# One block of each expert at fixed places first: the routed tail of a cross-attention and mixture-of-experts kernel

## The chip, the core and the metric

The kernel runs on one core of a Trainium2 chip. The metric is the device time of one execution in microseconds (us), as the median of several runs. Besides the runs there is one profiled execution, whose trace shows every instruction of the five engines: TensorE (PE), VectorE (DVE), ScalarE (ACT), GpSimd (POOL) and SyncE (SP), the last of which only issues transfers (DMA).

## The reference, cut to what matters

The reference is a layer over 8 images of 512 rows of width 256. A first half (cross-attention that keeps the top scores, a modulated long convolution, an MLP) gives a new `x`. The second half, which the change is about, is a mixture of 8 experts of which each row takes one, beside a shared expert:

```
logits = x @ gate_w                       # 8 experts
top_id = argmax(logits);  score = sigmoid(max(logits))
xs = x * score
y_e = (silu(xs @ rt_gate[e]) * (xs @ rt_up[e])) @ rt_down[e]     # only e = top_id is used
out = x_in + tanh(g_ffn) * (shared_swiglu(x) + y_{top_id})
```

Each expert has three weight matrices of 512 KB (`rt_gate`, `rt_up`, `rt_down`), all in float32.

## The kernel before, in words

**Recording and order.** The kernel does not issue its instructions as it is written. Calls go through proxies of the engines into a planner (`Plan`), which notes cost, inputs, outputs and buffers of each operation. `Plan.order()` then makes a greedy list schedule: at each step it takes the operation that can start first by its model, and among those ready the one noted earliest. That schedule is issued in one go, so the order on each engine, SP among them, is fixed when the kernel is built. All recorded instructions carry the helper's line L323; transfers that need a register carry the lines of their own functions.

**Stages.** For image `b`, `prepare` and `attention` run beside `behind(b - 1)`, which does `mixed` (the long convolution: products `pfi`, `pxf`, `pfo`, `py` on PE, with sums `yf` on POOL) and `after_mix` (the MLP of the first half, the router, the shared expert) of the image before. The last image has no attention beside it; `attended` is true from there on.

**The routed rows.** `after_mix` scatters the rows of an image, in four indirect transfers of 128 rows from POOL, into a table `xtab` in HBM in which every expert has its own stretch of `CAP` rows. `blocks_of` counts on DVE how many whole blocks of 128 rows each expert has that are not done yet (`pdone`), and writes for `TAKE[b]` blocks which expert (`blk[b][:, 0]`) and which first row (`blk[b][:, 1]`) each has. `block` then does one block. It loads 128 rows (`xb`, L1282, with a register for the first row, L1281) and three weight matrices (`load_w`, L1295, with a register for the expert, L1293), transposes the rows (`pxb`), multiplies (`pg`, `pu`), applies silu and product (`sgr`, `ger`), multiplies by `rt_down` (`pyr`), scales (`yb` on ACT), and adds the result to the rows of `out` with an indirect accumulating transfer from POOL (`out_dram<-yb,to`). Two such accumulations touch the same tensor, so each waits for the one before it to land. In `routed`, the `pyr` part of a block is put behind the first part of the next block.

**The end.** Image 6 leaves four blocks (called 6_0 to 6_3 below); 6_0 is put beside `mixed(7)`, the other three between the MLP and the shared expert of image 7. When image 7 is scattered, `blocks_of` with `all_` true rounds up, so that all rows left are covered, and the last 15 blocks (`TAKE[7]`) run alone. If more than 15 were needed (`few`), a general path at the end would do everything again. From `attended` on, the weights of a block don't go to the pool of five weight buffers but to the attention's buffers, which are free by then:

```
room = ((pq, "s"), (pk, "e"), (pk, "acc")) if attended else ((wpool, "w"),) * 3
```

`pq` has four buffers of the tag `s`, `pk` has two of each tag. So four gate matrices, two up matrices and two down matrices can be held.

Of the kernel before, what the change touches and what calls it, by code (L numbers as in the profile page):

```python
# [16 lines left out]
I32 = mybir.dt.int32  # L17
AF = mybir.ActivationFunctionType
ALU = mybir.AluOpType
# [3 lines left out]
P = 128  # L23
# [320 lines left out]
def tile_kernel(ctx: ExitStack, tc: tile.TileContext, a: dict, out: bass.AP):  # L344
    nc = tc.nc
    x, cx = a["x"], a["ctx_768"]
    B, T, D = x.shape
# [5 lines left out]
    NE, _, NI = a["L0_ffn_rt_gate"].shape  # L353
# [12 lines left out]

    CAP = B * T + P
    DX = D + 1  # L370
    NBLK = B * T // P + NE - 1
    FIRST = 1
    TAKE = {b: NF for b in range(FIRST + 1, B - 1)}
    TAKE[FIRST] = NF * (FIRST + 1) - 5
    TAKE[B - 1] = NBLK - 1 - sum(TAKE.values())

    const = ctx.enter_context(tc.tile_pool(name="const", bufs=1))
    wpool = ctx.enter_context(tc.tile_pool(name="wpool", bufs=5))
    pa = ctx.enter_context(tc.tile_pool(name="pa", bufs=1))
    pk = ctx.enter_context(tc.tile_pool(name="pk", bufs=2))  # L380
    pq = ctx.enter_context(tc.tile_pool(name="pq", bufs=4))
# [7 lines left out]
    plan = Plan(nc)  # L389
    V, S, GP, TE, SY = (plan.engine(n, e) for n, e in (  # L390
        ("DVE", nc.vector), ("ACT", nc.scalar), ("POOL", nc.gpsimd), ("PE", nc.tensor), ("SP", nc.sync)))
# [7 lines left out]
    def bank2(name):  # L399
        return bank(name, ps_ac, "ac")  # L400
# [135 lines left out]
    capse = const.tile([P, NE], F32, name="capse")  # L536
    blim = const.tile([P, 2, NBLK], F32, name="blim")
    tid = const.tile([P, B * NT], I32, name="tid")
    xtab = dr.tile([NE * CAP + P, DX], F32, name="xtab")

    cum = const.tile([P, NE], BF16, name="cum")
    pdone = const.tile([P, NE], F32, name="pdone")

    pre = const.tile([P, 4, 2 * NE], F32, name="pre")
    base = const.tile([P, NE + 1], F32, name="base")
    blk = {b: const.tile([P, 2, n], I32, name=f"blk{b}") for b, n in TAKE.items()}
    few = const.tile([P, 1], F32, name="few")
    free = const.tile([P, NE], I32, name="free")
    for t_ in (cum, pdone, pre):
# [2 lines left out]
    GP.memset(blim[:, 0], float(NE - 1))  # L552
    GP.memset(blim[:, 1], float(NE * CAP))

# [49 lines left out]
    def setup():  # L604
# [16 lines left out]
        GP.memset(zrow[:, D : D + 1].bitcast(I32), 1 << 20)  # L621
        q.dma_start(xtab[NE * CAP :, :], zrow)
        yield
# [9 lines left out]
        GP.tensor_scalar(iotap, ioc, float(P), None, ALU.mult)  # L633
        GP.tensor_scalar(capse, iota8, float(CAP), None, ALU.mult)
        GP.tensor_copy(iotab, ioc)
# [463 lines left out]
    def after_mix(b, s, between=()):  # L1099
# [11 lines left out]
        acc = accs(f"am{b}")  # L1111
# [46 lines left out]
        E = V if b == B - 1 else GP  # L1158
# [8 lines left out]
        V.tensor_tensor(oh, bc(iota8, 1, NT), bc(fx[:, 0], 2, NE), ALU.is_equal)  # L1167
        E.tensor_scalar(fx[:, 1], fx[:, 0], float(CAP), None, ALU.mult)

# [19 lines left out]
        for t in range(NT):  # L1189
            GP.indirect_dma_start(out=xtab[:], out_offset=bass.IndirectOffsetOnAxis(ap=ix_[:, t : t + 1], axis=0),  # L1190
                                  in_=hx[:, t, :], in_offset=None)
        if b in TAKE and not general:
            blocks_of(E, blk[b], TAKE[b], b == B - 1)
        yield

        acc = accs(f"ae{b}")
# [25 lines left out]
    def blocks_of(E, to, n, all_):  # L1222

        pc = bank(f"pcnt_{to.name}")
        TE.matmul(pc[:, :NE], ones16, cum, start=True, stop=True)
        w_ = pk.tile([P, 2, NE], F32, tag="bw", name=f"bw_{to.name}", bufs=1)
        nb, di = w_[:, 0, :], w_[:, 1, :]
        S.activation(nb, pc[:, :NE], AF.Copy, scale=1.0 / P)
        E.tensor_scalar(nb, nb, (63.5 if all_ else -63.5) / P, MAGIC, ALU.add, ALU.add)
        E.tensor_scalar(nb, nb, MAGIC, None, ALU.subtract)  # L1230
        E.tensor_sub(pre[:, 0, NE:], nb, pdone)
        for i in range(3):
            E.tensor_add(pre[:, i + 1, NE:], pre[:, i, NE:], pre[:, i, NE - 2 ** i : 2 * NE - 2 ** i])
        en, st = pre[:, 3, NE:], pre[:, 3, NE - 1 : 2 * NE - 1]
        if all_:
            V.tensor_scalar(few, en[:, NE - 1 :], float(n), None, ALU.is_le)
        V.tensor_scalar(en, en, float(n), None, ALU.min)

        E.tensor_sub(base[:, :NE], pdone, st)
        E.tensor_scalar(base[:, :NE], base[:, :NE], float(P), None, ALU.mult)  # L1240
        E.tensor_add(base[:, :NE], base[:, :NE], capse)
        E.tensor_sub(di, base[:, 1:], base[:, :NE])
        E.tensor_sub(nb, en, st)
        E.tensor_add(pdone, pdone, nb)
        cm = pk.tile([P, 2, n, NE], F32, tag="t2", name=f"cm_{to.name}")
        V.tensor_tensor(cm[:, 0], bc(iotab[:, :n], 2, NE), bc(en, 1, n), ALU.is_ge)
        E.tensor_mul(cm[:, 1], cm[:, 0], bc(di, 1, n))
        rd = pk.tile([P, 2, n], F32, tag="rd", name=f"rd_{to.name}", bufs=1)
        V.tensor_reduce(rd, cm, AX.X, ALU.add)
        E.tensor_scalar(rd[:, 1], rd[:, 1], base[:, 0:1], None, ALU.add)  # L1250
        E.tensor_add(rd[:, 1], rd[:, 1], iotap[:, :n])
        V.tensor_tensor(to, rd, blim[:, :, :n], ALU.min)
# [24 lines left out]
    def rows_of(bl, i, n, tag="xb"):  # L1277
        xb = pk.tile([P, DX], F32, tag=tag, name=f"xb{n}")

        def load():  # L1280
            r = nc.sync.value_load(bl[0:1, 1, i : i + 1], min_val=0, max_val=NE * CAP)  # L1281
            nc.sync.dma_start(xb, xtab[bass.ds(r, P), :])  # L1282

        plan.note_dma("SP", load, xb, [bl, xtab])
        return xb

    def block(bl, i, n, xb=None):

        if xb is None:
            xb = rows_of(bl, i, n)  # L1290

        def load_w(w, m):
            e = nc.sync.value_load(bl[0:1, 0, i : i + 1], min_val=0, max_val=NE - 1)  # L1293
            ap = a["L0_ffn_rt_" + m][bass.ds(e, 1)].rearrange("o k n -> (o k) n")
            nc.sync.dma_start(w, ap.rearrange("(c p) n -> p c n", p=P))  # L1295


        room = ((pq, "s"), (pk, "e"), (pk, "acc")) if attended else ((wpool, "w"),) * 3
        ws = []
        for m, k, (pool, tag) in zip(("gate", "up", "down"), (ND, ND, NIC), room):  # L1300
            t_ = pool.tile([P, 1024], F32, tag=tag, name=f"rt_{m}{n}")
            ws.append(t_.rearrange("p (c n) -> p c n", c=k))
            plan.note_dma("SP", partial(load_w, ws[-1], m), ws[-1], [bl])
        wg, wu, wd = ws
        to = pk.tile([P, 1], I32, tag="to", name=f"to{n}", bufs=3)
        GP.tensor_copy(to, xb[:, D : D + 1].bitcast(I32))
        p_ = bank(f"pxb{n}")
        for c in range(ND):
            TE.transpose(p_[:, c * P : (c + 1) * P], xb[:, c * P : (c + 1) * P], ident)
        xT = pk.tile([P, ND, P], F32, tag="xbT", name=f"xbT{n}")  # L1310
        S.copy(xT.rearrange("p c t -> p (c t)"), p_[:, : ND * P])
        p1, p2 = bank(f"pg{n}"), bank(f"pu{n}")
        for p_, w in ((p1, wg), (p2, wu)):
            for k in range(NIC):
                for c in range(ND):
                    TE.matmul(p_[:, k * P : (k + 1) * P], w[:, c, k * P : (k + 1) * P], xT[:, c, :],
                              start=(c == 0), stop=(c == ND - 1))
        sg = pk.tile([P, T], F32, tag="sg", name=f"sgr{n}")
        S.activation(sg, p1, AF.Silu)
        ga = pk.tile([P, T], F32, tag="ga", name=f"ger{n}")  # L1320
        V.tensor_mul(ga, sg, p2)

        def down():
            py = bank2(f"pyr{n}")
            for k in range(NIC):
                TE.matmul(py[:, :D], ga[:, k * P : (k + 1) * P], wd[:, k, :],
                          start=(k == 0), stop=(k == NIC - 1))
            yb = pk.tile([P, D], F32, tag="yb", name=f"yb{n}")
            S.activation(yb, py[:, :D], AF.Copy, scale=scal[:, 2:3])
            GP.indirect_dma_start(out=orows, out_offset=bass.IndirectOffsetOnAxis(ap=to, axis=0),  # L1330
                                  in_=yb, in_offset=None, bounds_check=B * T - 1, oob_is_err=False,
                                  compute_op=ALU.add)
        return down

    def routed(b, i0, i1, rows=None):
        late = None
        for i in range(i0, i1):
            now = block(blk[b], i, f"{b}_{i}", rows and rows[i])
            if late is not None:
                late()  # L1340
            late = now
            if i + 1 == i1:
                late()
            yield

# [12 lines left out]
    def together(*parts):  # L1358
        for _ in beside(*parts):
            pass  # L1360
# [12 lines left out]
    attended = general = False  # L1373
# [25 lines left out]
        pass  # L1399
    attended = True  # L1400
    together(behind(B - 1))
    together((routed(B - 1, 0, TAKE[B - 1]), 1))

    plan.issue(tc)

# [12 lines left out]
    with tc.If(rows_ok < P):  # L1418
# [10 lines left out]
        for b in range(B):  # L1429
            s = St()  # L1430
# [51 lines left out]
```

## Time and profile before

| | |
|---|---|
| median of 3 runs | 1792.7 us (1792.55 to 1793.37) |
| the profiled execution's own time | 1794.11 us |
| its span, first to last instruction | 1792.3 us |
| PE busy | 1513.1 us (84%) |
| DVE, ACT, POOL busy | 1302.1, 1154.6, 931.5 us |
| granted TensorE clock, mean | 0.874 |
| moved by DMA | 131.68 MB, mean 73 GB/s |
| DMA in the third last and second last of 40 slices | 228 and 280 GB/s |
| issues of rt_gate, rt_up, rt_down | 38 each, 512 KB |
| out_dram<-yb,to on POOL | 38 |

The shares of busy time are means over stages that are bound by different engines. The change works in the last 250 us of the span alone, so what counts is what ends last there: the table's whole-span figures only say how large that part is.

### The profile page before, as it was taken

The page shows a single profiled execution, that of the slowest core. Times are in us where ns is not written, and L with a number is a line of the kernel's source. Part 1 is how long each engine was busy: PE and PEld are TensorE (multiplying, and loading weights), DVE is VectorE, ACT ScalarE, POOL GpSimd, SP SyncE. Part 2 cuts the span into 40 slices and gives each one's busy share as a digit, 9 for nine tenths or more (in the row PEclk, how much of TensorE's full clock was granted, in tenths as well). Part 3 has the DMA queues.
Part 4 walks back from the last instruction along what each step waited for, and adds up shares of the span by engine and source line. Part 5 has one row for each costly group of instructions (what it writes and reads, how often), then busy time and mean ns, then how long its engine had stood idle before and what let it go on. Part 6 is the DMA issues. An engine that isn't in the chain of part 4 may idle for free. (4 is left out here: it accounts for less than half of the span.)

```text
span 1792.3 us, 21191 instructions
## 1 busy us (share of the span) xinstructions
PE 1513.1 (84%) x6363; PEld 893.1 (50%) x6363; DVE 1302.1 (73%) x3073; ACT 1154.6 (64%) x2008; POOL 931.5 (52%) x1072
## 2 busy tenths in 40 slices
PE   5365577797998798999889999998999989889885
PEld 2143333344543454465436554654465547547685
DVE  6989977885878697977798889697978987222210
ACT  4778844676747774887578877885788678123121
POOL 5578544445363645465555765474557646233122
PEclk8555677786998799998989999998999989989898
DMA  4000110001200120143103330431033205523794
GB/s 118 0 1 24 33 35 18 12 12 47 70 20 12 47 65 18 36 128 96 54 12 109 91 102 12 135 107 58 12 111 107 66 12 162 179 103 86 228 280 117
DMA packets 101289, 131.68 MB, mean 73 GB/s; under 512 B 9687, under 2 KB 73004, under 8 KB 101166
## 3 DMA queue, kind: packets, MB, share of 16 engines
q1 hardware_dynamic: 93102, 121.05, 21.1%
q0 software_dynamic: 7008, 8.42, 2.6%
q8 instruction: 52, 0.85, 0.2%
q10 hardware_dynamic: 1056, 0.79, 0.1%
q14 instruction: 71, 0.58, 0.1%
HBM read 112.22 MB, written 18.78 MB: 73 GB/s over the span
## 5 line engine op out<-in xcount | busy, mean ns | idle before, releaser
L323 PE MATMUL pS<-kT,qT 32*128 32x512 f32 x512 | 285.6, 742 | 71.2 <-DVE mn L323 61.0
L323 POOL TENSOR_TENSOR acc<-acc,e 128x1024 f32<-128x1024 f32 x96 | 229.0, 2385 | 182.3 <-ACT e L323 179.9
L323 DVE MAX8 top<-mn 128x8 f32<-128x256 f32 (+1 forms) x512 | 276.0, 556 | 11.9
L323 ACT COPY sc<-pS 128x512 f32<-128x512 f32 x256 | 145.6, 584 | 167.1 <-PE pS L323 136.9
L323 DVE SCALAR_TENSOR_TENSOR e<-sc,t,e 128x1024 f32<-128x1024 f32 x128 | 180.3, 1421 | 40.6 <-ACT e L323 40.3
L323 DVE TENSOR_TENSOR mn<-sc,pS 128x512 f32<-128x512 f32 x256 | 165.2, 677 | 35.9 <-PE pS L323 19.9
L323 POOL TENSOR_TENSOR mn<-mn 128x256 int32<-128x256 int32 x128 | 102.4, 800 | 164.4 <-DVE hi L323 163.8
L323 PEld LDWEIGHTS pS<-kT,qT 32*128 32x128 f32 x512 | 75.9, 208 | 203.6 <-DVE mn L323 98.9
L323 ACT ACTIVATE e<-sc,sm 128x1024 f32<-128x1024 f32 x128 | 145.1, 1146 | 16.1 <-POOL acc L323 13.2
L323 ACT ACT_TABLE_LOAD x118 | 151.4, 1283 | 4.0 <-issue 2.0
L323 PE MATMUL pm<-hT,w 128*128 128x512 f32 x256 | 137.9, 677 | 13.6 <-ACT hT L323 13.6
L323 ACT ACTIVATE junk<-sc,sm 128x1024 bf16<-128x1024 f32 x128 | 146.1, 1141 | 1.3
L323 PEld LDWEIGHTS pu<-aT,cx 128*96 128x96 f32 x1024 | 122.2, 168 | 28.6 <-issue 24.1
L323 PE MATMUL pu<-aT,cx 128*96 128x128 f32 x1024 | 135.4, 282 | 0.2 <-ACT aT L323 0.2
L323 PE MATMUL am<-w,ga 128*128 128x256 f32 x512 | 129.1, 398 | 6.1 <-ACT ga L323 6.1
L323 PEld LDWEIGHTS am<-w,ga 128*128 128x128 f32 x512 | 96.9, 196 | 51.4 <-issue 27.6
L323 POOL DMA_INDIRECT out_dram<-yb,to x38 | 61.5, 1620 | 96.7 <-DMA out_dram<-yb,to 46.3
L323 ACT ACTIVATE e<-e,sm 128x1024 f32<-128x1024 f32 x96 | 108.5, 1147 | 1.6 <-DVE sm L323 1.6
L323 POOL TENSOR_TENSOR mn<-mn,hi 128x256 int32<-128x256 int32 x128 | 104.9, 819 | 8.0
L323 DVE TENSOR_TENSOR ger<-sgr,pu 128x512 f32<-128x512 f32 x38 | 26.0, 684 | 108.7 <-PE pu L323 105.9
L323 DVE MATCH_REPLACE8 mn<-top,mn 128x256 f32<-128x256 f32 x256 | 104.6, 409 | 0.0
L323 POOL TENSOR_TENSOR yf<-yf,t 128x512 f32<-128x512 f32 (+1 forms) x80 | 85.2, 1089 | 35.0 <-DVE t L323 33.7
(287 smaller groups left out, 3125.0 us busy)
## 6 DMA issues: line engine op xcount, KB each, us to landing
rt_gate<-in_L_ffn_rt_gate_dram SPq DMA_DIRECT2D x38, 512.0 KB
rt_up<-in_L_ffn_rt_up_dram SPq DMA_DIRECT2D x38, 512.0 KB
rt_down<-in_L_ffn_rt_down_dram SPq DMA_DIRECT2D x38, 512.0 KB
w<-in_L_xattn_W_dram SPq DMA_DIRECT2D x32, 512.0 KB
cx<-in_ctx_dram SPq DMA_DIRECT2D x7, 768.0 KB
xtab<-zt SPq DMA_DIRECT2D x8, 642.5 KB
xb<-xtab SPq DMA_DIRECT2D x38, 128.5 KB
xt<-in_x_dram SPq DMA_DIRECT2D x8, 512.0 KB
```

The lines of the kernel that those rows point to most:

```text
L323: o.fn()
```

## The change

The 15 blocks at the end become 8 + 7. The first eight are one block for each expert, `own`: expert `e` at its first row not done yet, `pdone * P + e * CAP`. That is known when image 6 has been counted. Which expert comes when is fixed, so their weights are loaded by plain transfers without a register; only their rows need one. `pdone` goes up by one for each expert, `blocks_of` clips negative counts at zero, and the other seven blocks are routed as before. In every block after `attended`, the up and the down matrix now alternate between two tags (`e` and `mn`, `acc` and `kT`), so four of each can be held. This holds for the blocks 6_0 to 6_3 too, whose buffers come from the same tags.

```diff
-    TAKE[B - 1] = NBLK - 1 - sum(TAKE.values())
+    TAKE[B - 1] = NBLK - 1 - sum(TAKE.values()) - NE
...
+    own = const.tile([P, NE], I32, name="own")
...
         if b in TAKE and not general:
+            if b == B - 1:
+                V.scalar_tensor_tensor(own, pdone, float(P), capse, ALU.mult, ALU.add)
+                E.tensor_scalar(pdone, pdone, 1.0, None, ALU.add)
             blocks_of(E, blk[b], TAKE[b], b == B - 1)
...
         E.tensor_sub(pre[:, 0, NE:], nb, pdone)
+        if all_:
+            V.tensor_scalar(pre[:, 0, NE:], pre[:, 0, NE:], 0.0, None, ALU.max)
...
-            r = nc.sync.value_load(bl[0:1, 1, i : i + 1], min_val=0, max_val=NE * CAP)
+            first = own[0:1, i : i + 1] if bl is own else bl[0:1, 1, i : i + 1]
+            r = nc.sync.value_load(first, min_val=0, max_val=NE * CAP)
...
-        room = ((pq, "s"), (pk, "e"), (pk, "acc")) if attended else ((wpool, "w"),) * 3
+        room = ((pq, "s"), (pk, ("e", "mn")[i % 2]), (pk, ("acc", "kT")[i % 2])) if attended else ((wpool, "w"),) * 3
...
-            plan.note_dma("SP", partial(load_w, ws[-1], m), ws[-1], [bl])
+            if bl is own:
+                SY.dma_start(ws[-1], a["L0_ffn_rt_" + m][i].rearrange("(c p) n -> p c n", p=P))
+            else:
+                plan.note_dma("SP", partial(load_w, ws[-1], m), ws[-1], [bl])
...
     def routed(b, i0, i1, rows=None):
+        yield from blocks([(blk[b], i, f"{b}_{i}", rows and rows[i]) for i in range(i0, i1)])
+
+    def blocks(all_):
         late = None
-        for i in range(i0, i1):
-            now = block(blk[b], i, f"{b}_{i}", rows and rows[i])
+        for one in all_:
+            now = block(*one)
...
-    together((routed(B - 1, 0, TAKE[B - 1]), 1))
+    together((blocks([(own, e, f"o_{e}", None) for e in range(NE)]
+                     + [(blk[B - 1], i, f"{B - 1}_{i}", None) for i in range(TAKE[B - 1])]), 1))
```

More of the change, by code (lines that the diff above doesn't have):

```diff
@@ L1341, in routed @@
             late = now
-            if i + 1 == i1:
+            if one is all_[-1]:
                 late()
```

## The prediction

> **What bounds the kernel now.** The change touches nothing before image 7's own part, and the built orders of both kernels agree on every engine up to about 1536 us. So I read the end: first who waited for whom from 1680 us on, then SP's own waits, then POOL, PE and the stretches in order of time.
>
> ```profile
> POOL out_dram L323 <- DMA out_dram<-yb,to: 42.7, 9, 5.4
> PE pxb L323 <- DMA xb<-xtab: 8.2, 1, 8.2
> PE pyr L323 <- DMA rt_down<-in_L_ffn_rt_down_dram: 4.9, 4, 1.5
> ```
>
> ```profile
> SPq L1293 <- DVE blk L323: 23.1, 1, 23.1
> ```
>
> PE lost 8.2 us once, to the first rows of the last 15 blocks, and 4.9 us to `rt_down`. The longest wait is POOL's for its own accumulations. SP stood 23.1 us until `blk` was there. Now POOL in order of time:
>
> ```profile
> 1657.60 1.01 POOL L323 DMA_INDIRECT xtab<-hd,row  x1 [3.10 <-ACT hd L323]
> 1660.91 1.00 POOL L323 DMA_INDIRECT xtab<-hd,row  x1 [2.31 <-DMA xtab<-hd,row]
> 1664.48 0.96 POOL L323 DMA_INDIRECT xtab<-hd,row  x1 [2.57 <-DMA xtab<-hd,row]
> 1670.21 0.96 POOL L323 DMA_INDIRECT xtab<-hd,row  x1 [4.77 <-DMA xtab<-hd,row]
> ...
> 1719.19 1.57 POOL L323 DMA_INDIRECT out_dram<-yb,to  x1 [4.92 <-DMA out_dram<-yb,to]
> ...
> 1725.84 1.57 POOL L323 DMA_INDIRECT out_dram<-yb,to  x1 [4.88 <-DMA out_dram<-yb,to]
> ```
>
> The four scatters into `xtab` follow each other; the chain of waits has them landing after 2.53, 2.80, 4.96 and 6.38 us. The last two are slow because eight weight loads start at 1663.33, when `blk` lets SP go. The accumulations are a chain too: from one start to the next 6.65 us here, all of it issue and landing.
>
> ```profile
> 1558.78 0.44 PE L323 MATMUL pxb<-ident,xb 128*128 128x128 f32 x2 [4.00 <-DMA xb<-xtab]
> 1559.68 3.61 PE L323 MATMUL pg<-xbT,rt_gate 128*128 128x128 f32 x16 [0.46 <-ACT xbT L323]
> ...
> 1680.74 1.09 PE L323 MATMUL pxb<-ident,xb 128*128 128x128 f32 x4 [8.19 <-DMA xb<-xtab]
> 1681.86 3.79 PE L323 MATMUL pg<-xbT,rt_gate 128*128 128x128 f32 x16
> ...
> 1687.43 1.95 PE L323 MATMUL pg<-xbT,rt_gate 128*128 128x128 f32 x16
> ```
>
> ```profile
> 1675.00:1680.70 5.70, 0.00 (x0) 0.00 (x0) 0.00 (x0) 0.00 (x0) 0.04 (x1) 0.55 0.93 343
> 1680.70:1683.00 2.30, 2.23 (x9) 1.86 (x10) 0.00 (x0) 0.75 (x2) 0.33 (x2) 0.50 0.17 50
> 1700.00:1740.00 40.00, 36.83 (x276) 33.64 (x276) 4.13 (x6) 8.61 (x19) 11.55 (x13) 1.00 0.96 288
> 1765.00:1775.00 10.00, 10.00 (x70) 8.74 (x68) 1.38 (x2) 2.34 (x5) 2.32 (x3) 1.00 0.40 79
> ```
>
> After each long gap the clock (the column before the last two) is halved: 16 `pg` take 3.79 us, later 1.79 from one group to the next. From 1700 to 1740 the DMA engines are 0.96 busy at 288 GB/s. A block moves about 1.83 MB (three matrices of 0.524, rows of 0.13 in and out), so 6.3 us. PE needs 5.56 (from one `pg` to the next where nothing stalls, 1693.82 to 1699.38). The tail is bound by DMA and by the accumulations that share it, not by PE.
>
> **The change, part by part.** Time is summed against the profiled execution, 1794.1 us (span 1792.3 and 1.8 around it). The median of the runs, 1792.7, is 1.4 lower.
>
> *Blocks and rows: 0.* There are 15 blocks before and after. From the reference's inputs I counted the experts' rows (618 669 469 386 545 464 521 424): 14 blocks are left after image 6, six beyond one for each expert, so seven suffice and the general path stays off.
>
> *Three small DVE operations: +0.2.* They are 0.16 to 0.17 us each (`base`, `pre` rows at 1659 to 1660). `own` and `pdone + 1` stand ahead of 6's last count at 1536, which releases SP's first gate load: up to 0.2 on the path. The clip lies ahead of `blk`, which is needed eight blocks later.
>
> *The first `own` block's loads: 0.* In the built order its three loads stand ahead of the clearing transfers of `xtab`. Their buffers come free when 6_0 is through (1563 to 1568 before); DMA is idle from 1573 to 1583, and the clears wait for a later product anyway.
>
> *Block 6_0, moved: +2.8.* With four buffers each, `rt_up` of 6_2 and 6_3 and `rt_down` of 6_2 and 6_3 no longer wait for 6_0. SP's order now has these four loads ahead of 6_0's rows. DMA is full there (1.03 to 1.07 busy, 363 to 391 GB/s from 1543 to 1558), so 6_0's rows land 4 x 0.524 MB at 390 = 5.4 us later, at 1564.2 instead of 1558.8. The planner moves `pfi_3`, `pxf_0_0` and half of `pfo_0` ahead of 6_0 on PE, which fills to 1560.3; then PE stands 4 us as before and wakes at half clock. Behind 6_0 stand `pxf_0_1`, which ends near 1572.8 (before 1571.9), and then `pyr_0` ahead of the last two `pxf`, which end at 1578 instead of 1575.2. On POOL the accumulation of 6_0 moves from ahead of the `yf` sums to between them, 1.2 us. The sums end at about 1586.2 instead of 1583.4, and convolution, norm and MLP hang on them (PE waits 5.15 us for `hh` at 1595). Bounds: -1.5 if the rows land right behind the reordered products, +5 if each of these steps is a microsecond worse.
>
> *Own loads ahead of the scatters: -7.5.* Loads of `own` 1 to 3 are released as 6_1 to 6_3 leave their buffers, 1632 to 1648, and land by about 1652 (DMA is 0.24 to 0.29 busy there). Nothing in SP's order loads weights between then and the rows. So scatters three and four cost about what the first two did: 2.53 + 2.80 + 2.7 + 2.7, with three issues of 0.73, is 12.9 instead of 19.0. The rows behind them took 4.0 under load; quiet I estimate 2.5, from a scatter of the same 128.5 KB (2.53). 23.0 becomes 15.4. What is late next: the shared expert's last product, 1672.55, against rows at 1673. If that cover weren't there, nothing more could be gained. Bounds: -8.5 and -5.
>
> *The clock: -2.2.* PE's gap shrinks from 8.2 to about 0.5 us. Gaps of up to 1.5 us kept full clock (the `rt_down` waits from 1700 to 1740, clock 1.00). From the first `pxb` to the first `pyr` 10.3 us passed; at full clock it is 0.6 + 0.3 + 4 x 1.79 = 8.1. Bounds: -2.2 and 0.
>
> *The chain of 15 accumulations: 0.* Before, first to last start, 1694.18 to 1779.60, 14 links: 85.4 us.
>
> ```profile
> DMA to landing us min/median/max: 3.7/5.3/6.3
> ```
>
> A link is 1.0 of issue, the landing, and 0.35: the eight links from 1694 to 1752 that waited for DMA have a mean of 6.5, an idle one is 5.1. After, block k + 4's loads follow block k, so loads run through some 9.5 links and stop earlier: 9.5 x 6.5 + 4.5 x 5.25 = 85.4, the same. The `rt_down` stalls go (4.9 us), but what is late next is the accumulation: ACT has two `yb` buffers, so PE may lead by two blocks, no more. By volume it is the same: 33 loads instead of 37 in this phase, about 20.3 MB at 285 GB/s, end at 1752, three and a half blocks before the end.
>
> Here a rule speaks for more. The Trainium skill, "DMA: Bandwidth & Descriptors", section "Anatomy of one DMA — SWDGE (gpsimd) path", gives about 2.0 us and bytes over 436 GB/s for a transfer from GpSimd: 2.3 us for 128 KB, an estimate from the page. A link would be 3.7, PE's 5.56 would rule, and 14 x 5.56 = 77.8, 7.6 less. The row of this kernel has 3.7 at best and 5.3 in the middle, so I take the row and keep the rule's result as the lower end. The upper end is the slowest landing: 9.5 links of 7.65 instead of 6.5, +10.9. The same page, "Queues, rings and completion order", speaks against that: an engine takes turns between its queues packet by packet, so a deeper SP queue shouldn't lengthen a scatter that already shares with a full one.
>
> *Registers: 0.* 24 loads without one save some 0.75 us of SP each (0.45 instead of 1.2), but SP waits for buffers in this phase (8.7 us for `pg`, 7.6 for `pxb`).
>
> *Sum:* 0.2 + 2.8 - 7.5 - 2.2 + 0 = -6.7, so 1787.4 profiled and **1786.0** in the median.
>
> **The rivals.** *Chance 0.26: PE bounds the tail.* Weights are always four blocks ahead and landings shorten. For: `rt_down` stalls were real. Against: 288 GB/s at 0.96. -6.7 - 7.6: 1778.4.
>
> *Chance 0.14: the middle loses what the end gains.* Rows of 6_0 land still later, PE stands longer, and the convolution slips 8 us instead of 2.8: 1791.2. For: SP's order has the four loads ahead. Against: PE has 5 us of reordered work.
>
> *Chance 0.08, slower: the accumulations.* Loads that no longer pause keep each at the slowest landing, 7.65 a link: -6.7 + 10.9 = +4.2, 1796.9. It decides from a link of 7.2 on, where the gain is gone (6.7 over 9.5 links). For: landings up to 6.3. Against: DMA was 0.96 busy already.
>
> That the loads don't move is excluded by the built order, unless a release comes late; then the end is as before but for 6_0.
>
> **How the numbers follow.** The forecast has 0.52. Its own range is 1782 to 1790. Faster by over 0.2% (about what a measurement of this kernel can tell, 3.6 us, below 1789.1): nearly all of the forecast and the first rival, 0.76. Within: 0.15. Slower: 0.09. The range from 1777.5 to 1791.5 takes in the first two rivals.
>
> **What would show it.** Right: scatters into `xtab` all under 3 us, a gap under 2 us ahead of the first `own` block, `pg` there at 1.8 us, accumulation links near 6.5 and then near 5.2, `hh` about 2.8 us later. Wrong: `hh` more than 5 us later or earlier than before, scatters above 4 us, links at 5.6 (first rival) or above 7 (slower).

## The result and the profile after

The changed kernel takes 1786.24 us in the median (10 runs, 1781.26 to 1792.68), the kernel before 1793.03 (10 runs): a ratio of 0.9963, with a 95% interval of 0.995 to 0.9976. Measured once more on another occasion it was 1786.38 against 1793.19, 0.9958 (0.9941 to 0.9975). It is faster by 6.8 us; 1786.0 was predicted.

The profiled execution of the changed kernel took 1792.2 us (span 1790.5), 6 more than its own median. So its absolute times can't be laid beside those of before. I cut the end into four stages, each from one landmark to the next, and compare lengths: S1 from SP's first gate load of 6_0 to the first scatter into `xtab`, S2 to the first `pxb` of the last 15 blocks (`pxbo` in the changed kernel), S3 to the start of their first accumulation, S4 to the start of the last one. A second profiled execution of each kernel (their records are among the experiments) shows how far one execution is to be trusted.

| us | S1 | S2 | S3 | S4 | sum |
|---|---|---|---|---|---|
| before | 119.5 | 23.1 | 13.4 | 85.4 | 241.5 |
| before, second profile | 119.3 | 22.9 | 13.6 | 83.8 | 239.5 |
| after | 123.1 | 15.1 | 11.8 | 81.7 | 231.6 |
| after, second profile | 123.8 | 14.8 | 11.6 | 82.2 | 232.4 |

First POOL in order of time, for the changed kernel (start, duration, engine, line, operation; in brackets the idle time before it and what ended it):

```profile
1669.10 1.01 POOL L323 DMA_INDIRECT xtab<-hd,row  x1 [1.82 <-ACT hd L323]
1672.60 0.98 POOL L323 DMA_INDIRECT xtab<-hd,row  x1 [2.49 <-DMA xtab<-hd,row]
1676.04 0.96 POOL L323 DMA_INDIRECT xtab<-hd,row  x1 [2.46 <-DMA xtab<-hd,row]
1679.44 0.96 POOL L323 DMA_INDIRECT xtab<-hd,row  x1 [2.44 <-DMA xtab<-hd,row]
...
1740.24 1.57 POOL L323 DMA_INDIRECT out_dram<-ybo,too  x1 [4.61 <-ACT yb L323]
1748.39 1.57 POOL L323 DMA_INDIRECT out_dram<-yb,to  x1 [6.37 <-ACT yb L323]
1753.40 1.57 POOL L323 DMA_INDIRECT out_dram<-yb,to  x1 [3.25 <-ACT yb L323]
1756.97 1.57 POOL L323 DMA_INDIRECT out_dram<-yb,to  x1 [1.80 <-DMA out_dram<-yb,to]
```

All four scatters now follow each other at 3.4 to 3.5 us; before, the last one was held up by 4.77. The last two accumulations shown are 3.57 us apart: that is a link while the DMA engines are no longer full. Now PE in order of time:

```profile
1572.95 0.69 PE L323 MATMUL pxb<-ident,xb 128*128 128x128 f32 x2 [5.64 <-DMA xb<-xtab]
...
1680.44 3.62 PE L323 MATMUL ae<-sh_down,ge 128*128 128x256 f32 x16
1684.15 0.41 PE L323 MATMUL pxbo<-ident,xbo 128*128 128x128 f32 x2
1685.32 0.44 PE L323 MATMUL pxbo<-ident,xbo 128*128 128x128 f32 x2 [0.77 <-DMA xbo<-xtab]
1685.60 1.95 PE L323 MATMUL pgo<-xbTo,rt_gateo 128*128 128x128 f32 x16
```

The gap of 8.19 us ahead of the last 15 blocks is gone. The first `pxbo` starts as the shared expert's last product (`ae`) ends, with no wait, and 0.77 us are left for the second rows. Block 6_0, on the other hand, waits for its rows 5.64 us instead of 4.00, and at a later place. Who waited for whom from 1690 us on:

```profile
POOL out_dram L323 <- DMA out_dram<-ybo,too: 23.6, 5, 5.7
POOL out_dram L323 <- ACT yb L323: 18.0, 4, 6.4
...
ACT yb L323 <- DMA out_dram<-ybo,too: 3.8, 2, 2.9
...
PE pyr L323 <- DVE ger L323: 2.3, 4, 0.8
```

No wait of PE for `rt_down` or any other weight is left. POOL still waits longest, for its own accumulations. New is a wait of ACT for a `yb` buffer that an accumulation still reads, and of PE for `ger`. POOL's second row, put down to ACT's `yb`, needs a second look at ACT:

```profile
1747.71 0.47 ACT L323 ACTIVATE yb<-pyr,scal 128x256 f32<-128x256 f32 x1 [2.92 <-DMA out_dram<-ybo,too]
...
1771.65 0.47 ACT L323 ACTIVATE yb<-pyr,scal 128x256 f32<-128x256 f32 x1 [2.10 <-PE pyr L323]
```

The accumulation of 1740.24 lands after 7.4 us, at 1747.6. ACT waits for the same landing (its buffer comes free with it), ends a little later than the landing, and so gets the blame for POOL's 6.37 us ahead of 1748.39: it is a wait for an accumulation. Towards the end it is PE: the scaling at 1771.65 has waited for `pyr`, and so has the accumulation behind it.

SP no longer waits for `blk` ahead of the weights; its longest wait from 1660 us on is for the rows:

```profile
SPq L1290 <- DMA xtab<-hd,row: 20.9, 1, 20.9
```

Last the stretches (busy us and instructions of PE, PEld, DVE, ACT and POOL, granted clock, DMA share, GB/s):

```profile
1664.00:1684.00 20.00, 20.00 (x68) 11.54 (x66) 10.13 (x51) 7.01 (x12) 5.48 (x5) 1.00 0.17 41
...
1700.00:1740.00 40.00, 39.66 (x295) 36.40 (x293) 4.38 (x8) 9.92 (x22) 10.62 (x12) 1.00 0.99 304
1740.00:1755.00 15.00, 12.63 (x89) 11.24 (x90) 1.91 (x3) 2.89 (x6) 5.14 (x6) 1.00 0.89 289
1755.00:1778.00 23.00, 18.46 (x134) 16.51 (x132) 2.21 (x4) 4.59 (x10) 7.47 (x9) 1.00 0.15 24
```

While the scatters run, DMA is 0.17 busy at 41 GB/s and PE never stops, with full clock. Between 1700 and 1740 PE is busy 39.66 us of 40 (36.83 before) although DMA is fuller still, 0.99 at 304 GB/s. From 1755 on DMA is nearly empty.

### The profile page after: what moved, and what is told of

It is laid out like the page before. It is cut to its first block, busy times and chain, and to the rows that moved or that the text cites. A ratio compares the mean times of both kernels' runs of the same rounds, so it can differ in the third digit from the quotient of the medians.

```text
span 1790.5 us, 21072 instructions
## 1 busy us (share of the span) xinstructions
PE 1517.7 (85%) x6363; PEld 893.1 (50%) x6363; DVE 1302.9 (73%) x3076; ACT 1154.7 (64%) x2008; POOL 929.5 (52%) x1072
## 5 line engine op out<-in xcount | busy, mean ns | idle before, releaser
L323 PEld LDWEIGHTS pm<-hT,w 128*128 128x128 f32 x256 | 52.1, 213 | 79.2 <-issue 54.2
L323 DVE TENSOR_REDUCE hi<-mn 128x256 f32<-128x512 f32 x128 | 87.9, 687 | 0.0
```

The source lines that it names most:

```text
L323: o.fn()
```

## The experiments

Between them they split the change in its two halves (fixed blocks, more buffers), take the accumulations away, and then free PE from them step by step. Each is compared with the kernel before on the same chip. All stages in us, PE's stretch from the first `pg` (or `pgo`) to the end of the last `pyr`:

| | time, median | ratio to before, 95% | S1 | S2 | S3 | S4 | PE |
|---|---|---|---|---|---|---|---|
| before | | 1 | 119.5 | 23.1 | 13.4 | 85.4 | 93.3 |
| after | 1786.24 | 0.9963 (0.995 to 0.9976) | 123.1 | 15.1 | 11.8 | 81.7 | 87.9 |
| own_only | 1783.92 | 0.9948 (0.9928 to 0.9968) | 120.2 | 15.1 | 11.6 | 84.0 | 89.8 |
| buf_only | 1800.87 | 1.0028 (1.0014 to 1.0041) | 123.5 | 28.5 | 13.7 | 83.0 | |
| alt_late | 1782.13 | 0.9935 (0.9919 to 0.995) | 120.5 | 14.8 | 11.6 | 81.9 | 88.0 |
| no_acc | 1775.98 | 0.9896 (0.9875 to 0.9917) | 123.4 | 14.8 | 11.0 | | 83.6 |
| alt_late_yb4 | 1782.21 | 0.9944 (0.9925 to 0.9962) | 119.3 | 15.0 | 11.6 | 81.1 | 87.2 |
| alt_late_to8 | 1782.97 | 0.9932 (0.991 to 0.9954) | 120.1 | 15.8 | 11.7 | 81.6 | 83.2 |

**Fixed blocks without the buffers.** `own_only` is the changed kernel with the old `room` line:

```diff
-        room = ((pq, "s"), (pk, ("e", "mn")[i % 2]), (pk, ("acc", "kT")[i % 2])) if attended else ((wpool, "w"),) * 3
+        room = ((pq, "s"), (pk, "e"), (pk, "acc")) if attended else ((wpool, "w"),) * 3
```

> The eight own blocks come first, but a block's up and down matrix stay with one tag each, as in the kernel before (two of each held, four gates). Theory (the loss in the middle comes from the four loads that extra buffers let ahead of block 6_0's rows; the gain at the end from loads that are done before the scatters): from 6_0's first gate load to the first scatter into xtab as before, 119.5 us and not 123.1; eight own loads are early, so the four scatters and the rows take 15 us as with the change (23.1 before); the 15 accumulations take as long as before, some 85 us, since up and down run only two blocks ahead. Sum 0 - 8 - 1.7 + 0 = about -10: 1783 us. Rival (the extra buffers carry the end): scatters no faster than 19 us, 1790 us or more.

Measured: 1783.92 (6 runs, 1781.41 to 1791.62), with S1 back at 120.2 and S2 and S3 as in the changed kernel. So the gain ahead of the last blocks comes from the fixed blocks alone: their loads need nothing of `blk`, so they pass before the scatters. The buffers do nothing for it. What they are good for is seen in the waits of its last blocks, where PE still waits for down matrices:

```profile
PE pyr L323 <- DMA rt_down<-in_L_ffn_rt_down_dram: 2.8, 3, 1.4
...
PE pyro L323 <- DMA rt_downo<-in_L_ffn_rt_down_dram: 0.9, 2, 0.6
```

With the buffers S4 is about 2 us shorter (81.7 to 82.2 in the changed kernel, 84.0 here), and S1 is 3 us longer. In time `own_only` (0.9928 to 0.9968) can't be told from the changed kernel, nor from `alt_late` below: that the second half of the change pays at all is not shown.

**The buffers without fixed blocks.** `buf_only` is the kernel before with the changed kernel's `room` line.

> The kernel before with nothing but the two more buffers; no own blocks, all 15 as routed. Theory: the middle slips by 3.6 us as with the change. Twelve loads instead of eight start when the block table is there, so they collide with the scatters as before and stand ahead of the rows: from the first scatter to the first block 23.1 plus up to 4 loads of 1.4 = 23 to 29 us. The chain shortens by the 3.8 us seen with the change at most. Sum 0 to +6: 1793 to 1799 us. Rival (the buffers carry the gain): 1789 or less.

Measured: 1800.87 (12 runs, 1795.0 to 1804.07), slower, and 1.9 above the range that I had given. S2 is 28.5 us, 5.3 longer than before. PE in order of time:

```profile
1692.85 1.09 PE L323 MATMUL pxb<-ident,xb 128*128 128x128 f32 x4 [13.53 <-DMA xb<-xtab]
1693.97 3.79 PE L323 MATMUL pg<-xbT,rt_gate 128*128 128x128 f32 x16
```

The gap ahead of the rows has grown from 8.19 to 13.53 us, and PE starts at half clock behind it, as before (16 `pg` in 3.79 us). SP shows why: twelve weight loads now find a buffer when `blk` comes, where eight did, and the rows stand behind them in the same queue:

```profile
1682.04 0.37 SPq L1295 DMA_DIRECT2D rt_up<-in_L_ffn_rt_up_dram  x1
1683.24 0.38 SPq L1295 DMA_DIRECT2D rt_down<-in_L_ffn_rt_down_dram  x1
1684.23 0.39 SPq L323 DMA_DIRECT2D out_dram<-xr  x1
1685.46 9.75 SPq L1282 DMA_DIRECT2D xb<-xtab  x4
```

So by itself the second half of the change loses, for the same reason for which 6_0 loses in the changed kernel.

**The buffers for the last 15 blocks only.** `alt_late` is the changed kernel, but the blocks of image 6 keep one tag each:

```diff
+        k_ = i % 2 if bl is own or bl is blk[B - 1] else 0
-        room = ((pq, "s"), (pk, ("e", "mn")[i % 2]), (pk, ("acc", "kT")[i % 2])) if attended else ((wpool, "w"),) * 3
+        room = ((pq, "s"), (pk, ("e", "mn")[k_]), (pk, ("acc", "kT")[k_])) if attended else ((wpool, "w"),) * 3
```

> The change, with the two more buffers for up and down used by the last 15 blocks alone; blocks 6_0 to 6_3 keep the tags of before. Theory: 6_0's rows again stand ahead of the loads that wait for 6_0, so the first scatter comes 119.5 us after 6_0's first gate load (123.1 with the change); everything after it as with the change (15.1 to the first own block, 11.8 to the first accumulation, 81.7 for the chain). Sum about 3.6 less than the change: 1782.6 us. Rival (6_0's rows are not what slips): no better than the change, 1786.

Measured: 1782.13 (6 runs, 1780.8 to 1786.53). SP in order of time, `alt_late` first and then the changed kernel:

```profile
1538.45 0.39 SPq L1303 DMA_DIRECT2D rt_gate<-in_L_ffn_rt_gate_dram  x1
...
1551.17 6.02 SPq L1290 DMA_DIRECT2D xb<-xtab  x4
```

```profile
1546.02 0.39 SPq L1303 DMA_DIRECT2D rt_gate<-in_L_ffn_rt_gate_dram  x1
...
1560.28 3.18 SPq L1303 DMA_DIRECT2D rt_down<-in_L_ffn_rt_down_dram  x2
1563.51 1.46 SPq L323 DMA_DIRECT2D sh_gate<-in_L_ffn_sh_gate_dram  x1
1565.80 4.03 SPq L1290 DMA_DIRECT2D xb<-xtab  x4
```

The rows of 6_0 are issued 12.7 us after the first gate load here and 19.8 us after it there; `pxb` of 6_0 follows 21.7 and 26.9 us after it (before: 20.7). S1 goes from 123.1 to 120.5, while S2 to S4 stay as good. The order on PE around 6_0 is that of before again, too. So the four loads and the reordering that follows from them are shown as the cause together, not each by itself; nor was it tried how much of the delay is the transfer of the four matrices and how much SP's time to issue them. A repetition:

> The same kernel as alt_late, as the control for alt_late_yb4 on the same chip: about 1782 us, ratio to before 0.9935, stages as before (first scatter to first rows 14.8, accumulations first to last start 82).

It gave 1783.58 (8 runs), ratio 0.9958 (0.9939 to 0.9977), with S1 120.2, S2 15.0, S3 11.7 and S4 81.7: the stages repeat. The changed kernel, run beside it, had the same ratio, 0.9958, though a median 2.8 us higher (1786.38). So the 3 us of S1 are shown by the stages; in the time they are not clear of the spread.

**The changed kernel once more.**

> The changed kernel once more, for a second profiled execution. If the 7.8 us that the first one lost between 1389 and 1507 us (PE at 0.65 to 0.67 of its clock for 25 us) belong to that execution alone, this one loses nothing there, its own time is near the median of 1786, and the stages repeat: gate load of 6_0 to first scatter 123, first scatter to first rows 15, rows to first accumulation 11.8, first to last accumulation 82. If the stretch is the kernel's, it comes again.

Its profile took 1786.38 us, at the median, and the stages repeat within 0.7 us. Between two landmarks far ahead of anything that the change touches (the store of `xr` near 1389 us and the load `xo` near 1507) before needs 118.42 us, this one 118.72, and the first profile of after 125.87: 7.5 us more. The stretches of that first profile show the clock there:

```profile
1410.00:1420.00 10.00, 8.37 (x11) 2.64 (x10) 7.03 (x14) 5.47 (x9) 4.66 (x6) 0.65 0.01 2
1420.00:1430.00 10.00, 10.00 (x18) 3.54 (x17) 5.20 (x8) 2.79 (x5) 5.29 (x4) 0.67 0.00 0
```

In the second one the clock is 1.00 in both. So this loss belongs to the execution and not to the kernel. It is not the only one: the profile of `alt_late_again` has a clock of 0.67 from 1410 to 1420 and needs 121.73 us between the landmarks, where that of `alt_late`, the same kernel, needs 118.90.

**The kernel before once more.**

> The kernel before once more, for a second profiled execution of it. The stages of the changed kernel's two profiles add up to 9.9 and 9.1 us less than those of the one profile of before, the medians of the times to 6.8 less. If the first profile of before was drawn long in the end, this one has first scatter to first rows under 22 or first to last accumulation start near 83, and the four stages add up to about 239. If they repeat (119.5, 23.1, 13.4 and 85.4, in sum 241.5, within 1), the 2 to 3 us lie outside the stages, in how long the executions took before 1540 us.

The sum of its stages is 239.5, and it is S4 that is shorter, 83.8 instead of 85.4; the others repeat within 0.3. The first profile of before, on which the prediction was built, was drawn 1.7 us long in the accumulations.

**Without the accumulations.** In `no_acc` 14 of the last 15 are left out:

```diff
         def down():
...
             S.activation(yb, py[:, :D], AF.Copy, scale=scal[:, 2:3])
+            if bl is own and i or bl is blk[B - 1]:
+                return
             GP.indirect_dma_start(out=orows, ...)
```

> The change without 14 of the last 15 accumulations into out (their results are not written; all else is computed). Theory (the accumulations and PE share the bound of the tail): with the change the first pg of the own blocks to the last pyr took 87.9 us; without them PE runs at 5.56 us a block, 15 x 5.56 + 1.7 = 85.1, so PE ends 2.8 us earlier, and some 7 us of accumulations behind PE's end go as well: 10 us less than the change, 1776 us. Rival 1 (weight loads bound the tail): PE's stretch stays at 87.9, only the end behind it goes, 1779. Rival 2 (the accumulations alone set the pace): PE's stretch falls below 84.

Measured: 1775.98 (2 runs). PE's stretch is 83.6 us, no wait for a weight in it (its first and last lines, then a stretch of 40 us within it):

```profile
1678.45 1.95 PE L323 MATMUL pgo<-xbTo,rt_gateo 128*128 128x128 f32 x16
...
1759.02 3.01 PE L323 MATMUL pyr<-rt_down,ger 128*128 128x256 f32 x12
```

```profile
1700.00:1740.00 40.00, 40.00 (x304) 37.35 (x303) 4.81 (x7) 9.32 (x21) 1.28 (x7) 1.00 0.94 306
```

That is 15 x 5.57: PE at its own pace. My 85.1 counted the last `pyr` twice, and the limit of 84 that I had set for the rival came from the same slip, so it does not separate the two. What the run does show is that loads at 306 GB/s do not hold PE, which is busy all 40 us. Without the accumulations PE is 4.4 us faster (83.6 against 87.9); by which way they hold it comes next.

**Where the accumulations hold PE.** First guess: through the two `yb` buffers. `alt_late_yb4` gives them four:

```diff
-            yb = pk.tile([P, D], F32, tag="yb", name=f"yb{n}")
+            yb = pk.tile([P, D], F32, tag="yb", name=f"yb{n}", bufs=4)
```

> The changed kernel with the alternating buffers for the last 15 blocks alone, and four buffers of yb instead of two. Question: in no_acc PE ran the last 15 blocks in 83.6 us with no stall, in alt_late in 88.0, the 4.4 us being waits of ACT for a yb buffer that an accumulation still reads. Theory (the accumulations end the kernel, PE only follows them): PE's stretch from the first pg to the last pyr shrinks to 84 to 86 us, but the accumulations stay one behind the other, first to last start about 82 us; the time stays within 2 us of alt_late's 1782. Rival (PE, held by yb, sets the end): the time falls by PE's 4 us to about 1778.

Measured: 1782.21 (6 runs). ACT no longer waits for `yb`, and yet PE's stretch is 87.2: half of my expectation failed. PE's waits show what was left:

```profile
1724.48 0.70 PE L323 MATMUL pyr<-rt_down,ger 128*128 128x256 f32 x2 [0.85 <-DVE ger L323]
1730.69 1.99 PE L323 MATMUL pyr<-rt_down,ger 128*128 128x256 f32 x8 [0.42 <-DVE ger L323]
1733.51 2.05 PE L323 MATMUL pg<-xbT,rt_gate 128*128 128x128 f32 x16 [0.61 <-ACT xbT L323]
1738.20 1.13 PE L323 MATMUL pyr<-rt_down,ger 128*128 128x256 f32 x4 [0.63 <-DVE ger L323]
```

That is the order on PE: the planner has put `pyr` of some blocks right behind their own `pu`, where it has to wait for silu and product. By my reading its model makes the accumulations late, they hold one of three `to` buffers, and so it expects the next rows late. `alt_late_to8` gives `to` eight buffers, beside the four of `yb`, and the order becomes that of `no_acc`:

```diff
-        to = pk.tile([P, 1], I32, tag="to", name=f"to{n}", bufs=3)
+        to = pk.tile([P, 1], I32, tag="to", name=f"to{n}", bufs=8)
```

> alt_late_yb4 with eight buffers instead of three for `to`, the 128 row numbers of a block. In alt_late_yb4 nothing waited for yb any more, and still PE's stretch shrank only from 88.0 to 87.2 us: on PE the planner had put the pyr of blocks o_7, 7_0, 7_1 and 7_2 right behind their own pu, so that PE waited for silu and product (0.85, 0.42, 0.61 and 0.63 us), because by its model `to` is held by late accumulations and the next rows therefore come late. With eight of `to` the built order has every pyr behind the next block's first part, as in no_acc. Theory (PE's order sets the end, since the last accumulations follow PE at 5.55 us each): PE's stretch goes to 83.6 to 84.5, first to last accumulation start to 77.5 to 79, the time to about 1779. Rival (the accumulations under load set the end, 6.5 us for each of the first eight): PE's stretch shrinks the same, but the last accumulations are late and follow at 3.6 to 5 us each behind PE; first to last start stays at 80.5 to 82, the time at 1781 to 1783.

> Control for alt_late_to8 on the same chip: as alt_late_yb4, about 1782, PE's stretch 87.2, first to last accumulation start 81.

Measured: 1782.97 (8 runs) for eight `to`, 1782.48 (7 runs) for the control, whose stages were 120.3, 15.4, 11.7 and 81.5. PE's stretch fell to 83.2 us, its floor, and nothing came of it. PE and POOL of `alt_late_to8` in order of time:

```profile
1756.32 3.01 PE L323 MATMUL pyr<-rt_down,ger 128*128 128x256 f32 x12
```

```profile
1746.76 1.57 POOL L323 DMA_INDIRECT out_dram<-yb,to  x1 [4.26 <-ACT yb L323]
1750.31 1.57 POOL L323 DMA_INDIRECT out_dram<-yb,to  x1 [1.78 <-ACT sgr L323]
1754.27 1.55 POOL L323 DMA_INDIRECT out_dram<-yb,to  x1 [2.39 <-DMA out_dram<-yb,to]
1758.07 1.55 POOL L323 DMA_INDIRECT out_dram<-yb,to  x1 [2.25 <-ACT yb L323]
1762.69 1.55 POOL L323 DMA_INDIRECT out_dram<-yb,to  x1 [3.07 <-DMA out_dram<-yb,to]
1768.12 1.55 POOL L323 DMA_INDIRECT out_dram<-yb,to  x1 [3.89 <-DMA out_dram<-yb,to]
```

PE is through at 1759.33; the last accumulation starts 8.8 us later. In the control that lag is 4.6, in the changed kernel 4.0 (1773.54 to 1777.58). What PE gained became lag, and S4 stays at 81.6 (81.5 in the control): the theory (S4 77.5 to 79, 1779 us) failed, and the rival, that the accumulations under load set the end, held (S4 80.5 to 82, 1781 to 1783 us).

The links are not deaf to PE, though. The last five take 21.4 us here and 23.9 in the control. What cancels it is that the nine ahead of them, most of them under load, take 60.3 us here and 57.6 there. The loads come a little denser here (316 GB/s against 309 in the first 40 us of the chain), but that this makes the links longer is not shown. What is shown, by stages and time, is that 4 us less of PE do not shorten this end.

## Why the prediction was right, point by point

- **6_0, +2.8, and the DVE operations, +0.2.** S1 is 3.6 and 4.3 us longer than in the first profile of before. `pxb` of 6_0 moved 6.3 us (5.4 predicted from four loads at 390 GB/s), `hh` 4.8 and 5.1 us (2.8 predicted), counted from the first gate load. The mechanism is shown by `alt_late`: with the four loads no longer ahead of the rows, S1 is 120.5. The price was too low by about a microsecond. I had PE stand 4 us for the rows, and it stood 5.6; and `hh` is at the limit of 5 us that I had set for "wrong", in the second profile just past it.
- **Own loads ahead of the scatters, -7.5.** Measured -8.1 and -8.3. The scatters land after 2.5 to 2.7 us, as predicted (2.7), and what is late next is the shared expert, as predicted. `own_only` shows that this is the fixed blocks' doing, `buf_only` that it is not the buffers'.
- **The clock, -2.2.** S3 is 1.7 and 1.8 us shorter, with a granted clock of 1.00 and 16 `pgo` every 1.78 us. About half a microsecond less than forecast, 0.3 of it because the first rows come in two parts: from the first `pxbo` to the first `pgo` it is 1.45 us, where before it was 1.12. Clock and shorter wait were not tried apart.
- **The chain of 15 accumulations, 0.** This step failed in its size. I had the loads run through 9.5 links of 6.5 us and left 4.5 of 5.25: 85.4. Measured are eight links of a mean of 6.56 us (1695.92 to 1748.39) and six of 4.87 (1748.39 to 1777.58), together 81.7; in the second profile 6.55 and 4.97. The loaded link was right. How many of them there are was not, and my own two counts disagreed: 9.5 links are 61.8 us, while by volume the loads were to end at 1752, 57.8 us behind the first accumulation of before. The volume was right: the last weight load is issued at 1751.34, and the DMA engines are empty by about 1755, some 59 us behind the first accumulation. That is in the ninth and tenth link, and the ninth, in which the loads thin out (238 GB/s), already took only 5.0. So 1.5 links are short that I had counted as long (1.9 us), and six short ones are 0.4 us shorter than I had put them (2.3 us). Three of those six, 4.35, 5.98 and 5.58 us, end in a wait of ACT for `pyr`, and so for PE. The base was off too: 85.4 of one profile, 83.8 of the next. Between the four profiles the change of S4 is -1.5 to -3.8. A deeper queue of loads did not lengthen the link, as I had argued: the first eight have a mean of 6.43 us before and of 6.56 after.
- **The rule and the row.** The Trainium skill's 2.3 us for 128 KB from GpSimd ("DMA: Bandwidth & Descriptors", "Anatomy of one DMA — SWDGE (gpsimd) path", an estimate from the page) gave links of 3.7 us and a tail at PE's pace. With the DMA engines hardly loaded that nearly holds: there are links of 3.57 us in the changed kernel and of 3.55 in `alt_late_to8`, and the shortest landing is 2.8. Under load it does not; the landings in the last 15 blocks of the changed kernel (13 of them are in the trace) spread from near the rule to three times as much, the first eight blocks alone with a median of 5.5 us. The measurement decides, and the first rival, which rested on the rule, falls with it.

```profile
DMA to landing us min/median/max: 2.8/4.4/7.4
```

- **Rivals.** The middle did not lose what the end gains (S1 +4, not +8). The accumulations did not grow to 7.2 us a link. PE's stalls for weights went, as the first rival said, and three of the last links wait for PE, but PE did not become the bound of the tail: S4 is 81.7 and not 77.8, and `alt_late_to8` takes 4 us more off PE and the time stays.
- **Sum.** -6.7 predicted, -6.8 measured. That is closer than the steps deserve: the agreement to a tenth is luck. The two profiles of each kernel give stages of 240.5 before and 232.0 after in the mean, -8.5: the gains at the scatters and in the chain were larger than forecast (by 0.6 and 2.6 us), that of the clock smaller (0.4), 6_0 dearer (1.0). The 1.7 us between -8.5 and -6.8 are not settled: the eleven other profiles of these kernels reach SP's first gate load of 6_0 anywhere between 1534.0 and 1542.7, so that one or two profiles a kernel can't carry them.

The lowest medians of the kernels that compute everything belong to the changed one without the extra buffers for image 6, 1782.13 and 1783.58, and to its two variants with more `yb` and `to`; `own_only` (1783.92) is too near to be told from them.

## What to carry to other kernels

Loads that need no result of the stage before can pass ahead of its latency-bound small transfers; that was worth 8 us here (the saved registers were not tried by themselves). A buffer more is not free on an in-order queue: the loads that it releases stand ahead of whatever small transfer comes next, so give it only to the blocks whose next small transfer isn't waited for. (Here that took 3 us off S1.) Before freeing an engine from stalls, find what ends last behind it: 4 us less on PE came back as 4 us more lag of the accumulations.

## What the runs showed of the hardware

- In one execution the granted TensorE clock was 0.65 to 0.67 for 20 us while PE was busy 8.4 and 10 us of each 10 with hardly any DMA (1410 to 1430 us). Between its landmarks that execution took 7.5 us more; the second one of the same kernel had none of it, and one of another kernel (`alt_late_again`) half of it, 0.67 from 1410 to 1420. What sets it off is not shown.
- An accumulating indirect scatter of 128 KB landed after 2.8 us at best and 7.4 at worst within one tail: 4.4 to 7.4 in the first eight blocks, beside the weight loads, 2.8 to 4.2 behind them. Load is not all of it: in `alt_late_to8` the last link took 5.43 us with the DMA engines 0.14 busy; why is not shown. The first eight links had a mean of 6.43 us at 288 GB/s (before) and of 6.56 at 304 (changed).
